# Layer 1's pair sums: sums of both ways on two column tiles of 64, the 65th column on four tiles of 32

## The chip, the cores and the metric

The kernel runs on one core of a Trainium2 chip. The core has a matrix engine (TensorE, in the profile "PE", with its weight loads as "PEld"), a vector engine (DVE), a scalar engine for activations (ACT), a general engine (POOL) and a queue that issues most transfers (SP). They run side by side, each in the order of its own queue, and wait for one another by semaphores. The metric is the device time of one execution in microseconds, the median of several runs. Lower is better.

## The reference, cut to what matters

The program has four graph layers over 4096 nodes with 64 features and a 4096 x 4096 adjacency. The change touches layer 1 alone, a hyperbolic layer:

```python
adj_att = jax.nn.sigmoid(left[:, None] + right[None, :] + b_att[0]) * adj
x_local = logmap(x[:, None, :], x[None, :, :], c)
support_t = jnp.einsum('ij,ijd->id', adj_att, x_local)
return proj(expmap(x, support_t, c), c)
...
# --- layer 1 (adj_preln) ---
h = jnp.maximum(_layernorm(x, axis=-1), 0.0)
x = x + _L1_gnn_ref(h, adj, L1_gnn_r, L1_gnn_w_att, L1_gnn_b_att)
```

`logmap(x_i, x_j)` is a vector of 64, made of `x_i` and `x_j` with factors that depend on the pair alone. So the sum over `j` needs, for each target `i`, a weighted sum over all sources `j` of 65 columns: the 64 features of `x_j`, scaled, and one scalar of `j`. The weight of a pair is the sigmoid, zero where there is no edge, times a factor of the distance. That factor is the same for (i, j) and (j, i), the sigmoid is not.

## The kernel before, in words

Layer 1's pairs are computed by `pairs_fast` (from L2106). The 4096 nodes stand in 8 groups of 512. A job is a pair of groups (gi, gj) with gj <= gi: 36 jobs, 8 of them on the diagonal. Two jobs make a batch, so there are 18 batches. The steps of a batch are:

- `scores` (L2211): for each block of 128 sources, two matmuls into the PSUM tile `pl` (L2194 for the missing edges, L2197 for the logits) and a sigmoid on ACT into `sg` (L2181 by way of L2204). An off-diagonal job has both directions, that is 8 sigmoids of 128x512, a diagonal job has 4.
- `distances` (L2217): four fp32 matmuls into `pu` (L2225), each read by DVE into `at` (L2232), then one DVE operation over the job's whole tile into `xt` (L2233).
- `factors` (L2236): a table load (L2239), and per job four ACT passes over 128x2048 elements (the logarithm of `xt`, the root, its inverse, the logarithm of `at`) with two DVE operations, L2247 between the root and the logarithm and L2252 after it. The tile `root` has one buffer. At its end `at` holds the job's factor F: 4 blocks of 128 sources (of gj) by 512 targets (of gi).
- `sums` (L2254): DVE multiplies the weights `w` of the direction gj to gi by F (L2260). Four fp32 matmuls with 65 weight columns add this to `acci` (L2262), which is kept over all gj of one gi. For an off-diagonal job F is also transposed, 16 transposes of 128x128 (L2277) into four `pf` tiles (two buffers). DVE multiplies each with the other direction's weights (L2280), and a matmul adds it to `accj` (L2281). DVE then adds `accj` to the rows of `VT` (L2288). On the diagonal DVE copies `acci` to `VT` (L2270).

`VT` is 65 x 4096. `acci` and `accj` have one PSUM buffer each. At the end each 65x128 block of `VT` is transposed by TensorE (L2312) and scaled by DVE into `VQ` (L2314). `finish` then works on `VQ`.

The loop at L2294 issues, for batch n, the factors of batch n+1, the sums of batch n, the scores of batch n+1 and the distances of batch n+2. A scheduler orders each engine's queue from there. Only the activations are kept in program order (`act`, L2180). So on TensorE and DVE the work of neighbouring batches lies mixed.

In the trace an fp32 matmul has two weight loads and two passes (288 of each for the 144 matmuls of `acci`), and it is listed with as many weight columns as it has. Where the output is a slice of 32 partitions such as `acc[k * O : (k + 1) * O, :]`, as in layer 0 at L1521 and L1396, the trace lists matmuls of 32 columns. The sums of layer 1 use one accumulator of 65 partitions:

```python
nc.tensor.matmul(
    accs[gi],
    lhsT=XQ[:, gj * GB + b, :],
    rhs=w[:, b, :],
    start=(gj == 0 and b == 0),
    stop=(gi == gj and b == GB - 1),
)
```

Of the kernel before, what the change touches and what calls it, by code (L numbers as in the profile page):

```python
# [9 lines left out]
F32 = mybir.dt.float32  # L10
# [8 lines left out]
ALU = mybir.AluOpType  # L19
# [5 lines left out]
P = 128  # L25
N = 4096
NB = N // P
D = 64
G = 512
NG = N // G  # L30
GB = G // P
# [799 lines left out]
def kernel(  # L831
# [24 lines left out]
    nc = tc.nc  # L856
# [7 lines left out]
    D1 = D + 1  # L864
# [10 lines left out]
    ident = cpool.tile([P, P], F32, name="ident")  # L875
# [35 lines left out]
    def load_adj(apool, g, q):  # L911
# [6 lines left out]
        )  # L918
        return t

    def over(col, width):

        return col.unsqueeze(2).to_broadcast([P, col.shape[1], width])
# [75 lines left out]
    with ExitStack() as l0:  # L999
# [143 lines left out]
        @contextmanager  # L1143
        def in_order():

            traced = nc.cur_bb.bb.instructions
            mark = traced[-1]
            yield
            start = next(k for k in reversed(range(len(traced))) if traced[k] is mark) + 1
            last = {}  # L1150
            for i in traced[start:]:
                if i.engine in (nc.vector.engine, nc.scalar.engine, nc.tensor.engine):
                    if i.engine in last:
                        tc.add_manual_dep(
                            i,
                            last[i.engine].name,
                            mybir.DependencyInfo(
                                mybir.DependencyClass.NoSync, mybir.DependencyReason.DATA
                            ),
                            reason="in_order",  # L1160
                        )
                    last[i.engine] = i

        def staggered(*streams):

# [259 lines left out]
        with ExitStack() as ha:  # L1425
            hp = ha.enter_context(tc.tile_pool(name="heads", bufs=2))
            work = ha.enter_context(tc.tile_pool(name="hwork", bufs=1))
# [32 lines left out]
            for hf in range(2):  # L1460
# [9 lines left out]
                for hd in range(NH):  # L1470
# [61 lines left out]
                    for j0 in range(0, NB, 2):  # L1532
# [19 lines left out]
                        for i, j in enumerate(range(j0, j0 + 2)):  # L1552
                            for n, (acc, y) in enumerate(parts):
# [3 lines left out]
                                    lambda k, i=i: B[:, i, k * G : (k + 1) * G],  # L1557
                                    start=j == 0 and (n == 0 or acc is not parts[n - 1][0]),
                                    stop=j == NB - 1 and (acc is not accB or n == len(parts) - 2 - spatial),
                                )  # L1560
                        for i, j in enumerate(range(j0, j0 + 2)):
                            for c in range(2):
# [4 lines left out]
                                    lambda k, i=i: C[:, i, k * G : (k + 1) * G],  # L1567
                                    start=j == 0 and c == 0,
                                    stop=False,
                                )  # L1570
                                if whole:
# [534 lines left out]
    def pairs_fast(es, VQ):  # L2106
# [14 lines left out]
        with ExitStack() as ss:  # L2121
# [27 lines left out]
            for dst, k in ((XA, 0), (LD, 1)):  # L2149
# [11 lines left out]
                for g in range(NG):  # L2161
# [4 lines left out]
                        ps,  # L2166
                        nc.scalar.copy,
                    )
        VT = fp.tile([D1, N], F32, name="VT")
        work = es.enter_context(tc.tile_pool(name="pfwork", bufs=2))  # L2170
        with ExitStack() as ss:
            ps_u = ss.enter_context(tc.tile_pool(name="ps_u", bufs=2, space=PSUM))
# [4 lines left out]
            def grp(g):  # L2177
                return slice(g * G, (g + 1) * G)
# [57 lines left out]
            def factors(batch):  # L2236
# [12 lines left out]
                for job in batch:  # L2249
                    at, xt = tiles[job]  # L2250
                    act(at, at, AF.Ln, bias=one_t, scale=1.0)
                    nc.vector.scalar_tensor_tensor(at, at, TMAX, xt, ALU.min, ALU.mult)  # L2252

            def sums(batch):  # L2254
                for gi, gj in batch:
                    F_ = tiles.pop((gi, gj))[0]
                    if gj == 0:
                        accs[gi] = ps_a.tile([D1, G], F32, name="acci", tag="acci")
                    w = sig.pop((gi, gj))
                    nc.vector.tensor_tensor(w, w, F_, ALU.mult)  # L2260
                    for b in range(GB):
                        nc.tensor.matmul(  # L2262
                            accs[gi],
                            lhsT=XQ[:, gj * GB + b, :],
                            rhs=w[:, b, :],
                            start=(gj == 0 and b == 0),
                            stop=(gi == gj and b == GB - 1),
                        )
                    if gi == gj:
                        nc.vector.tensor_copy(VT[:, grp(gi)], accs.pop(gi))  # L2270
                        continue
                    w = sig.pop((gj, gi))
                    accj = ps_a.tile([D1, G], F32, name="accj", tag="accj")
                    for t in range(GB):
                        pf = ps_f.tile([P, G], F32, name="pf", tag="pf")
                        for b in range(GB):
                            nc.tensor.transpose(  # L2277
                                pf[:, b * P : (b + 1) * P], F_[:, b, t * P : (t + 1) * P], ident
                            )
                        nc.vector.tensor_tensor(w[:, t, :], w[:, t, :], pf, ALU.mult)  # L2280
                        nc.tensor.matmul(  # L2281
                            accj,
                            lhsT=XQ[:, gi * GB + t, :],
                            rhs=w[:, t, :],
                            start=(t == 0),
                            stop=(t == GB - 1),
                        )
                    nc.vector.tensor_tensor(VT[:, grp(gj)], VT[:, grp(gj)], accj, ALU.add)  # L2288


# [13 lines left out]
                    distances(batches[n + 2])  # L2304

        nc.vector.tensor_scalar(pabs, pabs, sqc, 2.0, ALU.mult, ALU.mult)
        with tc.tile_pool(name="ps_vt", bufs=2, space=PSUM) as ps:
# [406 lines left out]
```

## Time and profile before

| What | us |
|---|---|
| median of 3 runs | 2257.73 (2257.61 to 2261.93) |
| profiled execution | 2264.45 |
| its span, first to last instruction | 2262.7 |
| pairs of layer 1, from the first `pu` to the last `VQ` | about 1240 to 1832 |
| DVE work of `finish` that follows directly | from 1832.06 |

Over the whole span PE is busy for 1938.4 us (86%), DVE for 1770.1 (78%) and ACT for 1589.8 (70%). The other stages are layer 0 before the pairs, and layers 2 and 3 after them. The pairs are a bit over a quarter of the span, and nothing of another layer runs beside them: `finish` reads `VQ`, whose last block comes from the last job. The pairs hardly use transfers (57 loads of 256 KB between 1280 and 1830 us).

In the profile's lines an engine's group gives the line, the operation, output and input tiles with their shapes, the count, busy time and mean duration, and the idle time just before. Durations of matmuls overlap: a pass of 512 columns is listed with its way through the array, and the next pass starts before it is over. So the distance from start to start is the cost of a pass, and it is shorter than the duration.

### The profile page before, as it was taken

Reading aid. Unit: us, or ns where it says so; the run is one execution under the profiler, and the core shown is the slowest. Engines: PE = TensorE matmul, PEld = TensorE weight load, DVE = VectorE, ACT = ScalarE, POOL = GpSimd, SP = SyncE. Lnnn points to the kernel's source line nnn. Section 1 sums busy time; section 2 is a strip of 40 time slices with the busy share of each in tenths; the row PEclk is TensorE's granted clock in tenths of the full one; section 3 lists DMA queues with packets and bytes.
Section 4 is the critical chain, followed back from the end, with each engine's and each line's share of the span. In section 5 each row is a group of like instructions: output and inputs, shape, how many; then the busy total and the mean of one; then the engine's idle time right before and its main releaser. Section 6 shows DMA issues by size and latency. Waiting matters only on the chain. (4 is left out here: it accounts for less than half of the span.)

```text
span 2262.7 us, 42590 instructions
## 1 busy us (share of the span) xinstructions
PE 1938.4 (86%) x18732; PEld 904.9 (40%) x18732; DVE 1770.1 (78%) x2074; ACT 1589.8 (70%) x1338; POOL 86.0 (4%) x124
## 2 busy tenths in 40 slices
PE   4989989999999999859992799999999933959998
PEld 3444444444444544423441244434344411434332
DVE  6689989987898899797657888888898889544552
ACT  4678878996898899467752888879788920114775
POOL 1000100100000000001101000000000000000000
PEclk8999999999999999879995899999999966965999
DMA  9945554352111020477530001100110005724993
GB/s 112 181 89 104 90 90 114 123 190 93 44 63 63 26 75 2 132 247 264 188 122 20 20 23 33 38 24 28 33 33 26 26 0 204 301 82 140 332 332 119
DMA packets 117002, 238.92 MB, mean 106 GB/s; under 512 B 11059, under 2 KB 84003, under 8 KB 102051
## 3 DMA queue, kind: packets, MB, share of 16 engines
q1 hardware_dynamic: 101990, 192.92, 24.6%
q0 software_dynamic: 14816, 43.18, 10.8%
q8 instruction: 148, 2.42, 0.4%
q14 instruction: 48, 0.39, 0.1%
HBM read 245.34 MB, written 49.46 MB: 130 GB/s over the span
## 5 line engine op out<-in xcount | busy, mean ns | idle before, releaser
L1185 ACT ACTIVATE st<-srow,nt 128x2048 int8<-128x2048 f32 x352 | 682.8, 1994 | 81.6 <-DVE B L1191 80.8
L1191 DVE TENSOR_TENSOR B<-st,mres 128x1024 int32<-128x1024 int32 x256 | 312.0, 1221 | 71.8 <-PE accC L1521 44.6
L1521 PE MATMUL accB<-B,ybh 128*32 128x512 fp8e4 x3072 | 340.5, 385 | 15.6 <-DVE B L1191 15.6
L1521 PE MATMUL accD<-B,ybh 128*32 128x512 fp8e4 x2048 | 302.6, 388 | 23.6 <-DVE h L1637 23.6
L1521 PEld LDWEIGHTS <-ybh 128*32 128x32 bf16 (+1 forms) x6656 | 197.5, 98 | 240.8 <-issue 79.8
L1521 PE MATMUL accC<-B,ycn 128*32 128x512 fp8e4 x2272 | 267.8, 380 | 1.2 <-issue 1.2
L1521 PE MATMUL accC<-mres,ych 128*32 128x512 fp8e4 x2272 | 268.0, 381 | 0.0
L1521 PE MATMUL accL<-B,ybh 128*32 128x512 fp8e4 x1536 | 221.4, 391 | 4.8 <-DVE h L1641 4.7
L1521 PEld LDWEIGHTS <-ych 128*32 128x32 f16 x4096 | 169.0, 99 | 116.5 <-issue 11.9
L929 DVE SCALAR_TENSOR_TENSOR raw<-raw 128x2048 f32<-128x2048 f32 x64 | 146.4, 2289 | 79.3 <-DMA raw<-in_adj_dram 79.1
L1179 DVE TENSOR_SCALAR st<-srow,nt 128x2048 uint8<-128x2048 f32 x160 | 205.6, 1285 | 2.5
L2181 ACT ACTIVATE sg<-pl,rb 128x512 f32<-128x512 f32 x256 | 163.6, 684 | 53.7 <-PE pl L2197 50.6
L1185 ACT ACTIVATE st<-srowo,nto 128x1024 int8<-128x1024 f32 x128 | 137.3, 1137 | 42.1 <-DVE B L1191 42.1
L2225 PE MATMUL pu<-XAf,LDf 66*128 66x512 f32 x288 | 151.4, 630 | 13.7 <-DVE at L2232 12.5
L2607 ACT ACTIVATE w3b<-pv 128x1024 int16<-128x1024 f32 x128 | 131.1, 1024 | 45.6 <-PE pv L2598 45.3
L1521 PE MATMUL accC<-C,ych 128*32 128x512 fp8e4 x1824 | 148.3, 393 | 1.4 <-DVE C L1199 1.4
L1199 DVE TENSOR_TENSOR C<-B,mres 128x1024 int32<-128x1024 int32 x114 | 139.6, 1225 | 3.6
L2262 PE MATMUL acci<-sg,VQ 128*65 128x512 f32 x288 | 137.8, 602 | 4.8 <-DVE sg L2260 4.6
L1521 PEld LDWEIGHTS <-ycn 128*32 128x32 f16 x2272 | 107.6, 97 | 64.0 <-issue 3.1
L2416 PE MATMUL nacc<-m,HH 128*128 128x512 fp8e4 x256 | 62.0, 391 | 74.6 <-ACT HH L2405 74.6
L2232 DVE TENSOR_SCALAR at<-pu 128x512 f32<-128x512 f32 x144 | 95.2, 685 | 26.2 <-PE pu L2225 26.2
L2194 PE MATMUL pl<-nm,noid 128*128 128x512 fp8e4 x256 | 101.0, 395 | 11.8 <-ACT sg L2181 11.7
(488 smaller groups left out, 3124.3 us busy)
## 6 DMA issues: line engine op xcount, KB each, us to landing
raw<-in_adj_dram SPq DMA_DIRECT2D x64, 1024.0 KB, 6.9
mo<-edges SPq DMA_DIRECT2D x32, 512.0 KB, 4.7
noedge<-nmo POOLq DMA_DIRECT2D x32, 512.0 KB, 4.3
nm<-noedge SPq DMA_DIRECT2D x64, 256.0 KB, 3.1
m<-edges SPq DMA_DIRECT2D x16, 1024.0 KB, 5.2
m<-edges SPq DMA_DIRECT2D x32, 512.0 KB, 5.0
srow<-srow_d SPq DMA_DIRECT2D x15, 1024.0 KB, 6.6
mres<-in_adj_dram POOLq DMA_DIRECT2D x8, 1024.0 KB, 35.7
```

The costliest lines, as they stand in the source:

```text
L929: nc.vector.scalar_tensor_tensor(raw, raw, 0.0, raw, ALU.is_gt, ALU.not_equal, accum_out=bad[:, c : c + 1])
L1179: nc.vector.tensor_scalar(st[:, i, :].bitcast(U8), srow, negs[:, i : i + 1], EDGE, ALU.is_gt, ALU.mult)
L1185: nc.scalar.activation(st[:, i, :], srow, AF.Sign, bias=negs[:, i : i + 1], scale=-1.0)
L1191: nc.vector.tensor_tensor(B.bitcast(I32), st.bitcast(I32), edges.bitcast(I32), ALU.bitwise_and)
L1199: nc.vector.tensor_tensor(C.bitcast(I32), B.bitcast(I32), edges.bitcast(I32), ALU.bitwise_xor)
L1521: ins = nc.tensor.matmul(acc[k * O : (k + 1) * O, :], lhsT=values, rhs=moving(k), start=start, stop=stop,)
L2181: tc.keep_in_program_order(nc.scalar.activation(*args, **kw))
L2194: nc.tensor.matmul(pl, lhsT=noid, rhs=nm[:, b, :].bitcast(F8), start=True, stop=False)
L2225: nc.tensor.matmul(pu, lhsT=LD[:, j * P : (j + 1) * P], rhs=XA[:, grp(gi)], start=True, stop=True,)
L2232: nc.vector.tensor_scalar(at[:, b, :], pu, UMIN, None, ALU.max)
L2262: nc.tensor.matmul(accs[gi], lhsT=XQ[:, gj * GB + b, :], rhs=w[:, b, :], start=(gj == 0 and b == 0), stop=(gi == gj and b == GB - 1),)
L2607: nc.scalar.activation(w, pv, AF.Relu)
```

## The change

The sums are put on column tiles. `acci` and `accj` become 128 partitions high. The 64 features of one direction go to one half of the array's columns and those of the other direction to the other half: for `accj` to partitions 0 to 63, for `acci` to 64 to 127. The 65th column is computed by separate matmuls with 32 weight columns (the last 32 of the 65, of which only the last counts), at four places: for `accj` in partitions 64 to 95 and 96 to 127, for `acci` in 0 to 31 and 32 to 63, one each for the even and the odd source block. For two source blocks there are so 4 matmuls of 64 columns and then 4 of 32, and `in_order` keeps these eight in this order among TensorE's instructions (others may stand between them). An off-diagonal job issues such a group after every second transposed tile. Before, the `acci` matmuls of a job stood free of the transposed tiles. A diagonal job gives two of its four sources to `accj` and two to `acci`. Its four matmuls of 32 columns give the odd blocks to `acci` and the even ones to `accj`.

`VT` becomes 128 x 4096. On the diagonal two copies of 64 partitions (L2291 and L2292 of the changed kernel) bring `acci` to the halves where `accj` has them, and `accj` is then added there as well. At the end a matmul with a constant `fold_v` takes the place of the transpose: it picks the 64 columns and adds the two partitions that hold the 65th.

`in_order` is moved out of another function unchanged. The diff, cut to its core:

```diff
-        VT = fp.tile([D1, N], F32, name="VT")
+        VT = fp.tile([P, N], F32, name="VT")
...
+            def add_up(acc, low, row, src, w, start, stop):
+                cols, r, n = (slice(0, D), low, D) if row is None else (slice(D1 - 32, D1), row, 32)
+                nc.tensor.matmul(
+                    acc[r : r + n, :], lhsT=XQ[:, src, cols], rhs=w, start=start, stop=stop
+                )
...
                     if gj == 0:
-                        accs[gi] = ps_a.tile([D1, G], F32, name="acci", tag="acci")
+                        accs[gi] = ps_a.tile([P, G], F32, name="acci", tag="acci")
+                    acci = accs[gi]
+                    accj = ps_a.tile([P, G], F32, name="accj", tag="accj")
                     w = sig.pop((gi, gj))
                     nc.vector.tensor_tensor(w, w, F_, ALU.mult)
-                    for b in range(GB):
-                        nc.tensor.matmul(
-                            accs[gi],
-                            lhsT=XQ[:, gj * GB + b, :],
-                            rhs=w[:, b, :],
...
                     if gi == gj:
-                        nc.vector.tensor_copy(VT[:, grp(gi)], accs.pop(gi))
-                        continue
...
+                        with in_order():
+                            for b in range(0, GB, 2):
+                                j = gj * GB + b
+                                add_up(accj, 0, None, j, w[:, b], b == 0, b == GB - 2)
+                                add_up(
+                                    acci, D, None, j + 1, w[:, b + 1], gi == 0 and b == 0, b == GB - 2
+                                )
+                            for b in range(GB):
+                                j = gj * GB + b
+                                r = b // 2 * 32
+                                if b % 2:
+                                    add_up(acci, 0, r, j, w[:, b], gi == 0, True)
+                                else:
+                                    add_up(accj, 0, D + r, j, w[:, b], True, True)
+                        accs.pop(gi)
+                        nc.vector.tensor_copy(VT[0:D, grp(gi)], acci[D : 2 * D])
+                        nc.vector.tensor_copy(VT[D : 2 * D, grp(gi)], acci[0:D])
+                    else:
+                        v = sig.pop((gj, gi))
+                        for t in range(GB):
...
+                            nc.vector.tensor_tensor(v[:, t, :], v[:, t, :], pf, ALU.mult)
+                            if t % 2 == 0:
+                                continue
+                            with in_order():
+                                for c in range(t - 1, t + 1):
+                                    add_up(accj, 0, None, gi * GB + c, v[:, c], c == 0, c == GB - 1)
+                                    add_up(
+                                        acci, D, None, gj * GB + c, w[:, c], gj == 0 and c == 0, False
+                                    )
+                                for k in range(2):
+                                    c = t - 1 + k
+                                    last = c + 2 >= GB
+                                    add_up(accj, 0, D + k * 32, gi * GB + c, v[:, c], t == 1, last)
+                                    add_up(
+                                        acci, 0, k * 32, gj * GB + c, w[:, c], gj == 0 and t == 1, False
+                                    )
                     nc.vector.tensor_tensor(VT[:, grp(gj)], VT[:, grp(gj)], accj, ALU.add)
...
+        fold_v = work.tile([P, D1], F32, name="fold_v", bufs=1)
+        nc.vector.tensor_copy(fold_v[:, 0:D], ident[:, 0:D])
+        nc.vector.tensor_tensor(
+            fold_v[:, D:], ident[:, D + 31 : D + 32], ident[:, P - 1 :], ALU.add
+        )
...
-                    nc.tensor.transpose(pt[:, b, :], VT[:, c : c + P], ident[:D1, :D1])
+                    nc.tensor.matmul(
+                        pt[:, b, :], lhsT=VT[:, c : c + P], rhs=fold_v, start=True, stop=True
+                    )
```

More of the change, by code (lines that the diff above doesn't have):

```diff
@@ L919, in load_adj, with in_order @@
         return t
+    @contextmanager
+    def in_order():
+        traced = nc.cur_bb.bb.instructions
+        mark = traced[-1]
+        yield
+        start = next(k for k in reversed(range(len(traced))) if traced[k] is mark) + 1
+        last = {}
+        for i in traced[start:]:
+            if i.engine in (nc.vector.engine, nc.scalar.engine, nc.tensor.engine):
+                if i.engine in last:
+                    tc.add_manual_dep(
+                        i,
+                        last[i.engine].name,
+                        mybir.DependencyInfo(
+                            mybir.DependencyClass.NoSync, mybir.DependencyReason.DATA
+                        ),
+                        reason="in_order",
+                    )
+                last[i.engine] = i
     def over(col, width):
@@ L1141, in behind @@
                 yield
[L1143 to L1162, printed above, removed]
         def staggered(*streams):
@@ L2257, in sums @@
                     if gj == 0:
-                        accs[gi] = ps_a.tile([D1, G], F32, name="acci", tag="acci")
+                        accs[gi] = ps_a.tile([P, G], F32, name="acci", tag="acci")
+                    acci = accs[gi]
+                    accj = ps_a.tile([P, G], F32, name="accj", tag="accj")
                     w = sig.pop((gi, gj))
                     nc.vector.tensor_tensor(w, w, F_, ALU.mult)
-                    for b in range(GB):
-                        nc.tensor.matmul(
-                            accs[gi],
-                            lhsT=XQ[:, gj * GB + b, :],
-                            rhs=w[:, b, :],
-                            start=(gj == 0 and b == 0),
-                            stop=(gi == gj and b == GB - 1),
-                        )
@@ L2269, in sums @@
-                    if gi == gj:
-                        nc.vector.tensor_copy(VT[:, grp(gi)], accs.pop(gi))
-                        continue
[L2272 to L2287, printed above, removed]
+                    if gi == gj:
+                        with in_order():
[18 more added lines that the diff above has]
+                        for t in range(GB):
+                            pf = ps_f.tile([P, G], F32, name="pf", tag="pf")
+                            for b in range(GB):
+                                nc.tensor.transpose(
+                                    pf[:, b * P : (b + 1) * P], F_[:, b, t * P : (t + 1) * P], ident
+                                )
[15 more added lines that the diff above has]
+                                    )
@@ L2306, in pairs_fast @@
         nc.vector.tensor_scalar(pabs, pabs, sqc, 2.0, ALU.mult, ALU.mult)
+        fold_v = work.tile([P, D1], F32, name="fold_v", bufs=1)
+        nc.vector.tensor_copy(fold_v[:, 0:D], ident[:, 0:D])
+        nc.vector.tensor_tensor(
+            fold_v[:, D:], ident[:, D + 31 : D + 32], ident[:, P - 1 :], ALU.add
+        )
         with tc.tile_pool(name="ps_vt", bufs=2, space=PSUM) as ps:
@@ L2311, in pairs_fast @@
                     c = (g * GB + b) * P
-                    nc.tensor.transpose(pt[:, b, :], VT[:, c : c + P], ident[:D1, :D1])
+                    nc.tensor.matmul(
+                        pt[:, b, :], lhsT=VT[:, c : c + P], rhs=fold_v, start=True, stop=True
+                    )
                 bs = slice(g * GB, (g + 1) * GB)
```

## The prediction, made before the changed kernel was run

> **What bounds the kernel now.** I read the pairs of layer 1 alone, since nothing else changes, first by windows from one table load of ACT (L2239) to the next, one batch each. The columns are start and end, the length, then busy time and instructions of PE, PEld, DVE, ACT and POOL, the granted clock, and transfers.
>
> ```profile
> 1494.60:1532.60 38.00, 35.71 (x106) 14.68 (x105) 33.68 (x31) 28.33 (x27) 0.00 (x0) 0.91 0.10 28
> 1532.60:1563.80 31.20, 30.34 (x109) 13.40 (x108) 26.05 (x26) 28.11 (x27) 0.00 (x0) 1.00 0.12 34
> 1563.80:1593.70 29.90, 28.08 (x93) 12.11 (x92) 24.88 (x21) 25.82 (x23) 0.00 (x0) 0.94 0.09 27
> 1240.00:1832.00 592.00, 549.07 (x1792) 234.07 (x1792) 504.91 (x444) 488.44 (x438) 0.00 (x0) 0.95 0.10 29
> ```
>
> A plain batch takes 31.2 us and PE works through 30.3 of it. The batches around a diagonal job take 37 to 38 us, and there DVE has 33.7. All three engines are near their limit: 549, 505 and 488 us of 592. Next the waits from 1280 to 1830 us (engine, line, whom it waited for, us, times, longest):
>
> ```profile
> ACT sg L2181 <- PE pl L2197: 48.6, 90, 1.8
> DVE sg L2280 <- PE pf L2277: 24.3, 20, 2.2
> ACT xt L2181 <- DVE xt L2233: 20.6, 8, 4.4
> DVE VT L2288 <- PE accj L2281: 17.2, 11, 2.3
> ACT root L2181 <- DVE at L2247: 7.8, 17, 0.9
> ```
>
> PE is what the others wait for most: ACT in its sigmoids, DVE for transposes and finished sums. But a faster PE soon meets DVE. Then the groups of the change, same window:
>
> ```profile
> L2262 PE MATMUL acci<-sg,VQ 128*65 128x512 f32 x288 | 137.8, 602 | 4.8 <-DVE sg L2260 4.6
> L2281 PE MATMUL accj<-sg,VQ 128*65 128x512 f32 x224 | 109.0, 603 | 0.4 <-DVE sg L2280 0.4
> L2288 DVE TENSOR_TENSOR VT<-VT,accj 65x512 f32<-65x512 f32 x28 | 19.0, 679 | 17.2 <-PE accj L2281 17.2
> L2270 DVE COPY VT<-acci 65x512 f32<-65x512 f32 x8 | 5.5, 683 | 2.2 <-PE acci L2262 2.2
> ```
>
> The 512 passes belong to 256 matmuls. They overlap: in the timeline their weight loads follow every 0.429 us (1500.18, 1500.61, 1501.04), so a matmul costs 0.857 us.
>
> Last, whether fp32 matmuls on column tiles run side by side. Layer 0 has one such place, L1396: 8 fp32 matmuls with 32 columns, four to a PSUM tile (timeline: start, us, what).
>
> ```profile
> 42.23 1.92 PE L1396 MATMUL prs<-FT,rs 96*32 96x512 f32 x16
> ```
>
> Eight in a row would take 8 x 0.857 = 6.9 us. Their 16 passes take 1.92, which is four steps of 0.43 and the last one's way out. So four stand side by side, though each brings its two passes one behind the other. What it costs to change the tiling shows in layer 0's output stage:
>
> ```profile
> 1154.00 1.03 PE L1948 MATMUL acco<-B,YBo 128*128 128x512 fp8e4 x4
> 1154.87 1.03 PE L1948 MATMUL acco<-C,YCo 128*128 128x512 fp8e4 x4
> 1155.82 0.39 PE L1961 MATMUL ddo<-B,YD 128*32 128x512 fp8e4 x1
> ```
>
> Four passes of full width take 0.87 us, 0.216 each. From there to the first of 32 columns it is 0.95, that is 0.31 for the last step: about 0.095 us for the change. Back again it is the same (last narrow pass at 1151.95, first wide one at 1152.27).
>
> **What the Trainium skill says.** "TensorEngine Tiling (Array Packing)", Key Properties: changing the tiling mode drains the TensorE, and different tiles work in parallel. The trace agrees with both, with 0.095 us and with L1396. "TensorE: Matmul & The Clock Gate", Part 3, What overlaps and what doesn't: matmuls keep strictly to program order. If the second pass of the first tile held up the next tile, the eight of L1396 would need nine steps, some 4.0 us. They took 1.92, so the measurement decides. The same page, Part 1: an idle PE falls to half its clock. The trace agrees: in the batches with a diagonal job the clock is 0.91, in plain ones 1.00.
>
> **The change, part by part.** PE, from the order of the built program.
> (a) Removed: 256 matmuls x 0.857 = 219.4 us.
> (b) Added: 256 of 64 columns in 128 pairs, 128 x 0.857 = 109.7, and 256 of 32 columns in 64 fours, 64 x 0.857 = 54.8. In the built order all fours but one stand together, and at least 122 of the 128 pairs.
> (c) Added: changes of tiling. I count 253 in the built order, 4 to a group of eight. 253 x 0.095 = 24.0 us. No row here shows a change between 64 and 32 columns: it costs between 0 and 0.17 (the way out of a pass, 0.592 less 0.429). I take 0.095. This sets the sum between 18 and 29.
> (d) The fold of `VT`: 32 transposes at a step of 0.062 become fp32 matmuls with two passes of 0.111 (the step of L2621's 64 columns), +5.1 us, most of it beside other work.
> PE's demand falls by 219.4 - 164.5 - 24.0 - 5.1 = 25.8 us. Counted by steps (`pl` 0.216 a pass, `pu` 0.857, `pf` 0.109) its whole demand goes from 504 to 478 us of 592.
>
> DVE. The diagonal jobs get one more copy and one more add: 8 x 0.683 + 8 x 0.679 = +10.9 us, and `fold_v` well under 1. Height in partitions costs nothing extra (a 65 x 512 copy and a 128 x 512 operation, L2280, both take 0.68).
>
> Only waits count, so I follow ACT, whose order doesn't change. A batch of ACT has a stretch of factors (18.4 us in the timeline from 1563.8, with half a us idle) and a stretch of sigmoids.
>
> Sigmoids: ACT does two in 1.27 us, 0.635 each. PE has two `pl` ahead. I summed PE's work between a batch's third `pl` and its last in both built orders: 164.2 us before, 145.9 after, since fewer of the sums fall there and the `pu` spread differently. ACT itself needs 14 x 0.635 = 8.9 us (16 sigmoids) or 6.4 (12). What PE has above that, batch by batch, is 24.4 us before and 9.0 after: -15.4 us. This is half of the wait of 48.6; the rest is the start of each stretch, and stays.
>
> Factors: here the new order costs. In DVE's queue `VT` += `accj` stands ahead of a batch's first L2247 in 13 of 18 batches, in 7 before, and no more than 1.3 us of DVE's work lies between it and the last product with `pf`. PE needs after this product a pair, a four, two changes and the way out: 0.86 + 0.86 + 0.19 + 0.17, with 0.1 to notice, some 2.2 us. So DVE stands until about 7.0 us after the table load, then adds (0.7) and starts L2247 at 7.7. Before, it started at 6.9 (1570.74, table load at 1563.81). The next root has one buffer and waits for it: +0.7 us in the 6 batches where this is new, and some +0.5 in the other 7, where the add waited for a single matmul and now waits for a group: 4.2 + 3.5 = +7.7. Queued behind the waiting add is all of DVE. PE behind `accj` waits as before for DVE's products, now with no `acci` to fill in.
>
> Diagonal batches: DVE gets 1.36 us more, while PE's sums of the diagonal job fall from 3.43 to 2.57 + 0.29. Here ACT waits up to 4.4 us for `xt`, whose `pu` stood behind eight passes of `acci`. I set them against each other: 0, between -1.5 and +1.4 each, 8 of them. The tail after the last factor: PE -1.8, DVE's two more operations +1.4, the fold +0.5: 0.
>
> Sum: -15.4 + 7.7 + 0 = -7.7, say -8. Against the profiled execution of 2264.45 that is 2256.4. The median of the runs lies 6.7 us below the profiled one, so 2249.7.
>
> **The rivals.** R1, PE's relief gets through: the add costs no wait, and the diagonal batches speed up too, by 1 us each: -15.4 - 8 = -23, 2234; with half of it -15, 2243. For it: PE is the releaser of 102 us of waits. Against: ACT and DVE have 28.1 and 26.1 us of work in a 31.2 us batch, dependent on one another. R2, DVE takes over: its 10.9 us come in full, -15.4 + 7.7 + 10.9 = +3.2, 2261; no change if a little less. For it: 33.7 of 38 us in the diagonal batches. R3, slower: the add at the head of DVE's queue. In the built order 11 of the 36 adds have at most 0.68 us of DVE's work between the last product and themselves. At 2.2 us each stands 1.5, and so do the three ops of each diagonal job. If this reaches ACT in all 18 batches at 1.5 (27 us) with half of the diagonal's 10.9, and PE gives its 15.4: +17; with two thirds of it +11, 2269. It decides from a delay of about 1 us a batch. Against: 17.2 us of such waits exist already and go. R4, the tiles of 64 don't run side by side: 512 x 0.857 + 24 - 219 = +243, or some +90 if the second passes block. L1396 speaks against it, with 32 columns and not 64.
>
> **How the numbers follow.** A measurement of this kernel can tell 0.2%, 4.5 us. Chances: forecast 0.40 (own range 2240 to 2258), R1 0.11, R2 0.17, R3 0.27, R4 0.05. Faster by over 0.2%: 0.36 of the forecast and R1, 0.47. Within: 0.04 and 0.16, 0.20. Slower: R3, R4 and the rest of R2, 0.33. The range 2234 to 2272 leaves out R4, the end of R1 and the far part of R3, under 0.2. Signs of both kinds hold much of it.
>
> **What would show it.** Right: L2260's passes of the changed kernel start in twos and fours within hundredths of a us, and a group of eight takes about 2.9 us; the wait of ACT for `pl` falls from 48.6 to 30 to 36; plain batches take about 30.5 us. The step on the add is right if L2318's waits for `accj` don't fall below 17 and the root's wait for DVE grows by some 8. Wrong: passes one behind the other (R4), DVE's idle time gone in the diagonal batches (R2), or waits of DVE for `accj` above 30 (R3).

## The result, and the profile after

| | us |
|---|---|
| changed kernel, median of 12 runs | 2255.46 (2249.20 to 2267.20) |
| kernel before, beside it, 12 runs | 2258.03 (2244.47 to 2261.93) |
| ratio, from all runs and not from the medians | 1.0002 (95%: 0.9979 to 1.0025) |
| profiled execution of the changed kernel, its span | 2256.87, 2254.9 |

The forecast was 8 us faster. The runs show no difference. The profile shows one: its pairs are shorter. The windows from one table load of ACT to the next, for the three batches that were shown of before, and then the whole of the pairs (columns: start and end, length, busy time and instructions of PE, PEld, DVE, ACT and POOL, granted clock, transfers):

```profile
1486.60:1520.10 33.50, 29.77 (x117) 10.85 (x116) 31.28 (x28) 28.30 (x26) 0.00 (x0) 0.95 0.11 32
1520.10:1552.50 32.40, 31.66 (x145) 11.43 (x144) 28.14 (x25) 28.07 (x26) 0.00 (x0) 1.00 0.11 33
1552.50:1581.40 28.90, 27.21 (x134) 10.68 (x132) 26.01 (x25) 25.57 (x23) 0.00 (x0) 1.00 0.10 28
1232.40:1815.20 582.80, 532.80 (x2336) 201.12 (x2336) 514.86 (x461) 486.95 (x436) 0.00 (x0) 0.96 0.10 29
```

The batch around a diagonal job fell from 38.0 to 33.5 us, and the plain one rose from 31.2 to 32.4. PE's busy time fell by 16 us from the 549.07 shown of before (by 11 from the 544.26 of another profile of it, see below), and DVE's rose by the 10 us of the extra copies and adds. The waits of the changed kernel from 1270 to 1815 us (engine, line, whom it waited for, us, times, longest):

```profile
ACT sg L2183 <- PE pl L2199: 41.3, 77, 3.4
DVE VT L2318 <- PE accj L2260: 21.6, 11, 2.4
ACT root L2183 <- DVE at L2249: 16.6, 17, 1.9
ACT xt L2183 <- DVE xt L2235: 12.1, 5, 5.5
DVE sg L2301 <- PE pf L2298: 10.3, 21, 1.7
PE accj L2260 <- DVE VT L2318: 7.1, 5, 3.8
```

The root's wait for DVE more than doubled (7.8 before), `VT`'s for PE grew a little (17.2 before, and 14.1 to 15.3 in three more profiles of it), DVE's for `pf` fell (24.3). The last line is new: PE waits for the add to give `accj` free. The lines shown of before start some 25 us after the first table load and so leave out a part of ACT's wait for `xt`. From the first table load to the end of the pairs ACT waits as follows (us, from the third profiles of both kernels, see below):

| ACT waits for | before | changed |
|---|---|---|
| `pl`, in the sigmoids | 44.7 | 42.0 |
| `xt`, in the first logarithm | 24.1 | 12.1 |
| DVE's addition of the root, before the next root | 8.5 | 17.3 |
| all | 77.3 | 71.4 |

So the wait for `xt` is what got shorter, and the root's wait took most of that back. And here is one group in the timeline of the changed kernel (start, us, what), with a pair of 64 columns and a four of 32:

```profile
1525.28 0.64 PE L2260 MATMUL accj<-sg,VQ 128*64 128x512 f32 x1
1525.29 0.64 PE L2260 MATMUL acci<-sg,VQ 128*64 128x512 f32 x1
1525.76 0.59 PE L2260 MATMUL accj<-sg,VQ 128*64 128x512 f32 x1
1525.77 0.59 PE L2260 MATMUL acci<-sg,VQ 128*64 128x512 f32 x1
1526.29 0.62 PE L2260 MATMUL accj<-sg,VQ 128*32 128x512 f32 x1
...
1526.31 0.62 PE L2260 MATMUL acci<-sg,VQ 128*32 128x512 f32 x1
1526.74 0.59 PE L2260 MATMUL accj<-sg,VQ 128*32 128x512 f32 x1
...
1527.29 0.55 PE L2298 MATMUL pf<-ident,at 128*128 128x128 f32 x3
```

The tiles do stand side by side: both first passes start within 0.01 us, then both second ones. So what was to be found out is where the pairs' gain went.

### The profile page after: what moved, and what is told of

Read it like the earlier page. It is cut to its first block, busy times and chain, and to the rows that moved or that the text cites. A ratio compares the mean times of both kernels' runs of the same rounds, so it can differ in the third digit from the quotient of the medians.

```text
span 2254.9 us, 43716 instructions
## 1 busy us (share of the span) xinstructions
PE 1920.0 (85%) x19276; PEld 870.7 (39%) x19276; DVE 1780.3 (79%) x2092; ACT 1588.5 (70%) x1338; POOL 86.2 (4%) x124
## 4 chain that ended last, share of the span: by engine, by line
PE 34%; DVE 15%; DMA 6%; ACT 4%; issue 4%; POOL 0%; SPq 0%; DVEq 0%; POOLq 0%; ACTq 0%
PE accj L2260 6%; DMA raw<-in_adj_dram 5%; PE acco L1948 5%; PE pu L2227 3%; PE nacc L2453 3%; PE pl L2196 2%; PE pf L2298 2%; PE pl L2199 2%; DVE at L2249 2%; DVE raw L950 2%; PE accC L1521 2%; DVE at L2254 1%; PE ddo L1961 1%; PE accB L1521 1%; PE tr L982 1%
## 5 line engine op out<-in xcount | busy, mean ns | idle before, releaser
L2260 PE MATMUL accj<-sg,VQ 128*64 128x512 f32 (+1 forms) x512 | 198.3, 615 | 18.6 <-DVE VT L2318 7.1
L2260 PE MATMUL acci<-sg,VQ 128*64 128x512 f32 (+1 forms) x512 | 197.7, 615 | 0.0
L2183 ACT ACTIVATE sg<-pl,rb 128x512 f32<-128x512 f32 x256 | 163.1, 684 | 47.3 <-PE pl L2199 43.3
L2644 ACT ACTIVATE w3b<-pv 128x1024 int16<-128x1024 f32 x128 | 131.1, 1024 | 54.6 <-PE pv L2635 54.3
```

The lines of the kernel that those rows point to most:

```text
L2183: tc.keep_in_program_order(nc.scalar.activation(*args, **kw))
L2260: nc.tensor.matmul(acc[r : r + n, :], lhsT=XQ[:, src, cols], rhs=w, start=start, stop=stop)
L2644: nc.scalar.activation(w, pv, AF.Relu)
```

## The experiments

Each theory bears the name that the expectation of its run gives it. They were named anew for each set of runs.

**Side by side needs the order.** Here `in_order` is left out in both places of `sums`, everything else is as in the changed kernel.

```diff
-                        with in_order():
+                        if True:
...
-                            with in_order():
+                            if True:
```

> The changed kernel without the fixed order of the eight matmuls of a group; the scheduler orders them freely. In the built order most matmuls of one accumulator then stand alone between others, and the tiling changes 423 times and not 253. Theory 1 (the matmuls gain only where both halves are issued together): the passes of a lone matmul take 0.86 us and not half of it, PE's demand grows by about 50 to 110 us and the pairs take 610 to 690 us. Theory 2 (the hardware brings halves together across other matmuls in the queue): the pairs take less than 590 us.

Measured: 2440.84 us, ratio 1.0847 (1.0821 to 1.0872), the pairs 767 us from the first table load instead of 569. Timeline:

```profile
1525.56 2.06 PE L2260 MATMUL accj<-sg,VQ 128*64 128x512 f32 x6
1527.55 0.66 PE L2298 MATMUL pf<-ident,at 128*128 128x128 f32 x4
1528.13 1.04 PE L2260 MATMUL acci<-sg,VQ 128*32 128x512 f32 x2
```

Most passes come without a partner. The first line shows both cases: it is one lone matmul of 64 columns (two passes 0.48 us apart) and then two of 32 that still found each other (they are printed as one group, under the shape of the first). Counted by starts within 0.03 us of each other, 394 of the 1024 passes have a partner here and 990 in the changed kernel. The pairs are even longer than the 610 to 690 us that were expected. The two passes of one matmul of 32 columns take 0.98 us alone (1528.13 to 1529.11), no less than one of full width with a change of tiling. A narrow matmul isn't cheaper by itself; only a neighbour makes it so.

**The add at the head of DVE's queue.** A rule of order puts a batch's first `VT` += `accj` behind the first `at` += `root` of the same stretch.

```diff
+                    r = nc.vector.tensor_tensor(at, at, root, ALU.add)
+                    if job == batch[0]:
+                        roots.append(r.ins)
...
+                    a = nc.vector.tensor_tensor(VT[:, grp(gj)], VT[:, grp(gj)], accj, ALU.add)
+                    if (gi, gj) == batch[0]:
+                        tc.add_manual_dep(
+                            a.ins,
+                            roots[-1].name,
...
+                                mybir.DependencyClass.NoSync, mybir.DependencyReason.DATA
```

> The changed kernel with one edge more on DVE: the add of accj to VT of a batch's first job is issued behind the first addition of the root (L2249 of the changed kernel), and not ahead of it. Theory 1 (the add at the head of DVE's queue delays the root and with it ACT, the +7.7 us of the prediction): ACT's wait for that addition falls from 15.9 us to 6 to 9, DVE's wait for accj from 21.6 to under 15, and the pairs get 4 to 9 us shorter than the 569.1 of the changed kernel. Theory 2 (the delay only moves: accj is then free later, and PE's next group waits for the add): ACT's wait falls, PE's wait for the add grows from 14 us to 20 or more, and the pairs stay within 3 us of 569.

Measured: 2255.89 us, ratio 1.0015 (0.9982 to 1.0047), the pairs 573.4. The waits, same columns as above:

```profile
DVE sg L2304 <- PE pf L2301: 27.9, 27, 2.5
PE accj L2263 <- DVE VT L2321: 19.6, 16, 3.8
ACT root L2183 <- DVE at L2250: 18.1, 17, 1.8
```

DVE no longer stands in front of the add: its wait for `accj` falls from 21.6 us to under 4. But the root's wait, which both theories had falling, stays (18.1), PE's wait for the add, which frees the one `accj` buffer, grows from 7.1 to 19.6, and DVE's for `pf` from 10.3 to 27.9. The delay moved, it didn't go, and in this one profile the pairs are 4 us longer than in the changed kernel.

**DVE's extra work on the diagonal.** In one kernel the add of `accj` on the diagonal is left out, so half of the diagonal jobs' sums is missing from `VT`. In the other the two copies run on ACT.

```diff
-                    nc.vector.tensor_tensor(VT[:, grp(gj)], VT[:, grp(gj)], accj, ALU.add)
+                    if gi != gj:
+                        nc.vector.tensor_tensor(VT[:, grp(gj)], VT[:, grp(gj)], accj, ALU.add)
```
```diff
-                        nc.vector.tensor_copy(VT[0:D, grp(gi)], acci[D : 2 * D])
+                        nc.scalar.copy(VT[0:D, grp(gi)], acci[D : 2 * D])
...
```

> The changed kernel without DVE's add of accj on the eight diagonal jobs: half of the sources of the diagonal's own group are left out of the sums. DVE has 5.4 us less to do. Theory 1 (DVE decides in the batches with a diagonal job, the rival in which DVE takes over): the pairs get 5 us or more shorter, 564 or less. Theory 2 (PE's order and ACT's chain decide there): 567 to 570.

> The changed kernel with the two copies of acci to VT on the diagonal done by ACT in place of DVE. DVE has 10.9 us less, ACT some 9 more. Theory 1 (DVE decides in the batches with a diagonal job): the pairs take 560 to 565 us. Theory 2 (ACT's chain decides): they take 572 to 580, since the copies stand in ACT's queue ahead of its factors. The total within 0.3% of before either way.

Without the add the pairs took 572.5 us in its one profile, 3 us more than with it and more than either theory had: the pairs don't wait for this add, half of DVE's extra work. (Its time of 2247.64 comes from layer 3, with 213.4 us; see below.) With ACT's copies: 2281.14 us, ratio 1.0130 (1.0077 to 1.0183), the pairs 593.8. The groups of that run, us busy and ns of one before the last bar:

```profile
L2183 ACT ACT_TABLE_LOAD x37 | 47.5, 1283 | 3.3 <-PE pl L2199 2.6
L2291 ACT COPY VT<-acci 64x512 f32<-64x512 f32 x8 | 4.7, 582 | 10.3 <-PE acci L2260 10.1
```

The copies themselves are short. But in the timeline sigmoids now stand among the logarithms and roots (at 1501.19 us, 1509.72 and 1516.93, each between two table loads), and L2183 has 37 table loads where the changed kernel has 18: 19 x 1.283 = 24.4 us, all of the loss. So the run says nothing on DVE, and the copies, the other half of its extra work, stay untested; it prices a torn stretch of activations.

**The same two kernels again.** Both unchanged, twice more, for the spread of the profiles.

> The kernel before, run and profiled once more, to see how much its stages vary by themselves. Theory A (the pairs really are 8 to 9 us shorter in the changed kernel, and the rest of the program varies by as much on its own): the pairs, from ACT's first table load of the pairs to the first operation of the step after them, take 577 to 578 us again, while layer 0 and layer 3 move by several us against the first profile. Theory B (layer 3 is longer in the changed kernel because of the change): layer 3 takes 224 to 226 us again. Theory C (the pairs vary by themselves): the pairs are off 577.6 by 4 us or more.

> The changed kernel once more. Theory A: the pairs take 568 to 570 us again and layer 3 anything from 222 to 236. Theory B: pairs 568 to 570, layer 3 233 us or more again. Theory C: pairs off 569.1 by 4 us or more. Total within 0.3% of before in A and B.

> The kernel before, profiled a third time. So far its pairs took 577.6 and 573.9 us with 65 and 55 us at half clock, layer 3 took 224.1 and 222.9. Theory A (the pairs of before are 4 to 9 us longer than those of the changed kernel): 573 to 578 again. Theory C (the pairs vary with the clock's windows, and the two profiles fell on the long side): under 572.

> The changed kernel, profiled a third time. So far its pairs took 569.0 and 569.2 us, layer 3 took 233.2 and 227.3 with 73 and 64 us at half clock from its start to the end of the record. Theory A with a chance clock in layer 3: pairs 568 to 570, layer 3 may be 223 to 226. Theory B (layer 3 is longer because of the change): layer 3 227 or more again.

Measured: before 2252.69 and 2246.80 (ratios to the kernel before beside it 0.9998 and 0.9984), changed 2252.91 and 2254.14 (0.9997, 0.9992, to at most 1.0025). By stages, in us, each in the order first, second, third profile. The pairs are from the first table load, which comes 13.5 to 13.8 us after the first `pu`, to `finish`:

| stage | before | changed |
|---|---|---|
| start to first `pu` | 1240.9, 1239.9, 1239.3 | 1232.4, 1233.4, 1232.5 |
| pairs | 577.6, 573.9, 573.8 | 569.0, 569.2, 569.7 |
| `finish` and layer 2 | 206.5, 206.4, 206.3 | 206.5, 206.5, 206.5 |
| layer 3, from its first `pv` | 224.1, 222.9, 226.2 | 233.2, 227.3, 230.7 |
| span | 2262.7, 2256.5, 2259.1 | 2254.9, 2249.8, 2252.8 |

The first row differs by more than the pairs do, 7.2 us between the means, though nothing was changed there. In the other profiles below and above it is 1231.4 to 1235.2 for kernels made from the one before and 1236.2 to 1239.7 for those made from the changed one, so the change doesn't move it; what does is open. The spans can't be compared as wholes.

The pairs are shorter in each profile of the changed kernel, and the profiles, but not the runs, say that the kernel is faster. The 166 runs of before, over all its measurements, explain this: they fall into two heaps, 74 around 2247.1 and 92 around 2260.0, with few near 2253. All three profiles of before are of the upper one. The 39 runs of the changed kernel can be read as one heap around 2255.2 and four runs from 2237.8 to 2246.9; the gap between them is 2.4 us, and with the cut at 2253 that divides the runs of before, 15 of the 39 would be below. The means of all runs are 2254.2 and 2253.8, a difference of -0.4 (95%: -2.5 to 1.7).

**What makes the diagonal batches shorter.** Two kernels from the one before. The first puts a diagonal job's first `acci` matmul behind the last `pu` traced ahead of it. The second traces the distances of batch n+2 ahead of the scores of batch n+1, where that has a diagonal job.

```diff
+                        if gi == gj and b == 0:
+                            tc.add_manual_dep(
+                                m.ins,
+                                last_pu[-1].name,
...
+                                    mybir.DependencyClass.NoSync, mybir.DependencyReason.DATA
```
```diff
                 sums(batch)
+                early = more and any(gi == gj for gi, gj in batches[n + 1])
+                if early and n + 2 < len(batches):
+                    distances(batches[n + 2])
                 if more:
                     scores(batches[n + 1])
-                if n + 2 < len(batches):
+                if not early and n + 2 < len(batches):
                     distances(batches[n + 2])
```

> The kernel before, with one more rule of order on TensorE: a diagonal job's first matmul of acci stands behind the last pu of the distances traced just before it. No work is added or left out. In the traces the four batches that hold a diagonal job's sums (periods from one table load to the next of 35.8, 38.1, 37.9 and 37.2 us in the kernel before, 32.9, 33.5, 33.4 and 33.0 in the changed one) carry the whole gain of the change. Theory D (place: ACT's logarithm waits for xt because the last two pu stand behind acci's passes): where the rule moves pu ahead, in the periods of 38, the period falls by 2 to 4 us each, the pairs as a whole by 4 to 9 us. Theory E (amount: TensorE has less to do for a diagonal job in the changed kernel, and its place doesn't matter): the pairs stay within 1.5 us of 573.8. Time of the whole: by D 0.1 to 0.4% below before, by E no difference.

> The kernel before, with the distances of batch n+2 traced ahead of the scores of batch n+1 where batch n+1 holds a diagonal job; nothing else. So the scheduler takes pu ahead of pl there. Theory D: the waits of ACT for xt fall from about 20 us to under 10, and the pairs by 4 to 9 us, unless the sigmoids, now behind pu, give it back (then the wait of ACT for pl grows by as much). Theory E: the pairs don't get shorter; with the sigmoids later they get 5 to 15 us longer.

The first: 2256.25 us, ratio 1.0009 (0.9983 to 1.0034), the pairs 576.4; of the two periods of 38 us one became 38.9 and one 36.1. ACT's wait for `xt` over the pairs is 23.3 us, 24.1 before: the rule hardly took it away, so this run doesn't say what the place is worth. The second is the telling one. Its diagonal batch and the two that follow, and two of its waits:

```profile
1486.00:1518.40 32.40, 30.12 (x88) 12.40 (x89) 27.39 (x25) 28.23 (x27) 0.00 (x0) 0.89 0.11 33
1518.40:1549.60 31.20, 30.21 (x108) 13.46 (x109) 26.68 (x26) 28.11 (x27) 0.00 (x0) 1.00 0.12 34
1549.60:1585.20 35.60, 33.57 (x107) 14.20 (x107) 30.96 (x27) 25.74 (x23) 0.00 (x0) 0.95 0.08 23
```
```profile
ACT sg L2181 <- PE pl L2197: 65.4, 88, 3.5
...
ACT xt L2181 <- DVE xt L2233: 1.0, 1, 1.0
```

The wait for `xt` went from 20.2 us to 1.0, and the diagonal batch is 5.7 us shorter, more than the change brought. But the sigmoids now wait 65.4 us for `pl`, 21 more, a later batch has 35.6 us instead of 28.3, and the pairs are at 575.5 as before. So here the place decided which batch pays, and the sum stayed: what Theory D named as its exception, and what Theory E says of the pairs, though not the 5 to 15 us more that E expected. That the changed kernel gains by the smaller amount of PE's work fits this, but no run changed the amount alone. Nor is the clock kept apart from it: TensorE is at half clock for 54.6 to 64.9 us of the pairs in the four profiles of before and for 47.8 to 51.2 in the three of the changed kernel. The 8.8 us between the means are worth at most 4.4 us of PE's work, and may be a cause of the shorter batches or follow from them. The median of the second kernel is nevertheless 2246.73, ratio 0.9975 (0.9957 to 0.9993), with unchanged pairs: 18 of its 22 runs are below 2252, in the lower heap.

**What the heaps are.** One more profile of the kernel before.

> The kernel before, unchanged, for one more profile. Its runs fall into two heaps, around 2246 and around 2259 us, and all three profiles so far are of the upper one. Theory C (the end of the program meets the clock differently from run to run): if this one is of the lower heap, the pairs are again 573 to 575 us and layer 3 is shorter by about 10 us (near 213 to 216 instead of 223 to 226), with less time at half clock there. Theory A (the pairs vary): the pairs are shorter by about 10 us and layer 3 is as before. If it falls into the upper heap it tells nothing new.

It was of the lower heap: 2249.8 us, span 2248.1, the pairs again 575.2, layer 3 217.2. Layer 3's first 50 us in three profiles: first before in the upper heap, then before in the lower one, then the changed kernel (windows, columns as above; the number after POOL is the clock):

```profile
2032.90:2082.90 50.00, 50.00 (x161) 24.44 (x160) 21.08 (x28) 20.48 (x36) 0.00 (x0) 0.50 0.42 148
```
```profile
2030.90:2080.90 50.00, 49.43 (x225) 22.31 (x228) 24.13 (x31) 31.92 (x47) 0.00 (x0) 0.84 0.60 214
```
```profile
2021.70:2071.70 50.00, 50.00 (x161) 24.50 (x160) 21.10 (x28) 20.50 (x36) 0.00 (x0) 0.50 0.42 147
```

PE is listed as busy nearly all the time in each, but at half clock it gets through 161 passes instead of 225, and ACT with it through 36 activations instead of 47. In the records of the clock this stretch at half speed begins 42 us ahead of layer 3's first `pv` and lasts 92.2 us in the upper heap and 58.0 in the lower one, in nothing between. It is 92.2 in all three profiles of the changed kernel, also in the one of 2251.72 us; of all the kernels here those profiled at 2247.5 to 2249.8 us have 58.0. From its beginning on TensorE has only small matmuls (17.9 of the 42 us ahead of layer 3), of which the last is shown, and then nothing (timeline of the changed kernel, the bracket is the idle time before):

```profile
1999.53 1.97 PE L2513 MATMUL pz<-w2f,cT 128*128 128x64 f32 x8 [0.67 <-ACT cT L983]
2018.70 1.01 PE L2571 MATMUL plate<-cnt,lat 128*128 128x512 bf16 x2 [17.21 <-issue]
```

The stretch isn't all of the distance between the heaps. From the mean of the first three profiles of before to the fourth the span falls by 11.3 us: 7.2 of it in layer 3 and 4.8 ahead of the first `pu` (1240.0 to 1235.2, with 163.8 us at half clock there in place of 174.1 to 180.9), while the stages between take 0.7 more. There is one profile of the lower heap of this kernel.

**The stretch, made shorter.** The changed kernel with 80 more matmuls there, whose result nobody reads:

```diff
+            warm = ps.tile([P, G], F32, name="warm", tag="misc")
+            for k in range(80):
+                nc.tensor.matmul(
+                    warm, lhsT=cnt16[:, 0, 0:P], rhs=cnt16[:, k % 2], start=True, stop=True
+                )
             w3 = lp.tile([D, D], F32, name="w3f")
```

> The changed kernel, with 80 more bf16 matmuls of 128x128 by 512 columns at the end of layer 2, whose result nobody reads (operands are the edge counts, the output a PSUM tile of layer 3's pool). In the built order 36 of them lie between the small matmuls of layer 2's last groups and 44 in the 17 us in which TensorE stands still ahead of layer 3. Nothing else is changed. In the profiles so far one stretch at half clock begins some 42 us ahead of layer 3's first pv and lasts either 92.2 us (all three profiles of the changed kernel, the long ones of before) or 58.0 us (the short one of before, with a layer 3 of 217.2 us in place of 223 to 226). Theory C (this stretch, and nothing in the pairs, makes the heaps, and eats the change's gain in layer 3): with TensorE kept at work the stretch is 58 us or shorter, layer 3 is at most 217 us in place of 227 to 233, the two heaps become one, and the median lies at 2235 to 2245, below before by 0.5 to 0.8%. Theory B (layer 3 is longer because of the change itself or of its transfers): layer 3 stays at 225 us or more whatever the clock ahead of it, and the median stays within 2250 to 2260, or gets up to 5 us longer by what the added matmuls delay in layer 2.

Measured: 2234.35 us (2230.05 to 2238.47 in 6 runs), ratio to the kernel before 0.9916 (0.9886 to 0.9946). The kernel before, beside it, took 2252.25 us in 11 runs. Its windows of the 42 us ahead of layer 3 and of the first 50 of it:

```profile
1978.20:2020.20 42.00, 31.82 (x192) 18.57 (x193) 29.62 (x61) 8.07 (x20) 4.00 (x6) 0.91 0.24 89
2020.20:2070.20 50.00, 49.43 (x225) 22.37 (x228) 25.09 (x32) 31.90 (x47) 0.00 (x0) 0.83 0.62 219
```

The stretch is 23.9 us long and begins 7.4 ahead of layer 3. Layer 3 takes 213.3 us, layer 2 with `finish` 199.2 instead of 206.5 (its eight passes `pz` take 1.08 us instead of 1.97), and the pairs are as they were, 569.8. The gap isn't quite filled: 43 of the matmuls take 9.4 us of it, then TensorE stands still for 7.7 us, and in these the stretch begins.

Theory B, that layer 3 is longer whatever the clock, is out. Of Theory C the stretch and layer 3 came as expected, the median just below its range. Two parts of it aren't shown. Six runs, within 8.4 us, can't tell that two heaps became one. And the kernel before wasn't run with these matmuls, so how much of the 0.84% is the change's own, and whether the stretch had hidden the change's gain, isn't measured. By the profiles the pairs are some 5 us of it (569.8 against 575.1 before).

## Why the prediction came out as it did

- **Side by side** (step (b), R4): right. A group of eight with nothing between took 2.86 us (1494.39 to 1497.25 in the third profile), 2.9 were forecast.
- **PE's relief of 25.8 us**: too large, by the term (c), the changes of tiling. From start to start, each pass counted at most with its own length, the sums fell from 223.2 to 196.8 us. But (third profiles) `pl` rose by 5.6, `pf` by 5.4 and the fold by 4.7, and `pu` fell by 1.1: together -11.8. Over the 164.5 us of steps of (b), the changed sums take 32.3 more, and with `pl` and `pf` 43.3, or 0.17 for each of the 253 changes instead of 0.095. Some of this is PE's way out ahead of a wait, so it is an upper value. The prediction had bounded the change at 0.17 and taken the middle.
- **The sigmoids, -15.4**: at most half of it came. ACT's wait for `pl` is 41.2 to 42.0, not 30 to 36. It was 48.6 in the profile that the forecast was made from, but 45.0 and 44.7 in the next two, and from these the fall is some 3 us. (The fourth shows 41.7, with 30 of the 512 `pl` passes missing from its record and 5 us of such waits put down to others.)
- **The add, +7.7**: right in size. The root's wait rose by 8.8, `VT`'s stayed between 17 and 30 (21.6). What the step didn't say is that the delay has no better place: one `accj` buffer ties the add, PE and `pf` together.
- **The diagonal batches, 0**: wrong, and this is where the pairs' gain came from. By periods from one table load to the next (third profiles), four of the eight took 149.0 us before and 132.9 after. The other four, three near the start and the last, took 5.4 us more together, and the ten batches without sums of a diagonal job 6.6 more, where some -0.7 for a plain batch was expected. Over the pairs ACT's wait for `xt` fell by 12.0 us. The pushed `pu` was named in the step, and then set off against DVE's two operations; leaving out one of these gained nothing.
- **The clock**: the prediction took the 0.91 of a diagonal batch for what an idle PE does. That batch shows half clock beside pauses and no more: PE's longest pause in it is 1.86 us, and the third row of its windows, with no sums of a diagonal job, has 0.94.
- **The sum for the pairs, -8**: measured -5.8 (means of the four profiles of before, 575.1, and three of the changed kernel, 569.3). It was near by luck: the sigmoids gave far less than forecast, the diagonal batches gave what was set at 0, and the two offset one another.
- **From the pairs to the time**: this step failed, and with it the gain of the whole. The prediction read the pairs "alone, since nothing else changes", and took the 6.7 us between profile and median as a constant. Three runs and one profile gave that constant, and all four happened to lie in the upper heap. In the profiles layer 3 is on average 230.4 us after and 224.4 before, with the same instructions: of the upper heap both, with some 10 us more at half clock later in the layer (63.4 to 72.8 us in layer 3 against 55.6 to 58.9). And by the times, with the four low runs taken as its lower heap, the changed kernel is in that heap in 4 of 39 runs, the one before in 74 of 166. So counted it is 4.8 us faster within the upper heap (2255.2 against 2260.0), about what its pairs gained.

No difference had a chance of 0.20, as the near end of R2 and of the forecast. It came from neither: leaving out one of DVE's extra operations gained nothing, and R3's delay cost what the forecast had given it. If the changed kernel meets the longer stretch more often, as the times suggest, why it does isn't settled. The starts of layer 3 at 2021.7 to 2022.6 us (changed) and 2030.9 to 2038.6 (before) don't order the cases: one kernel with 2027.2 and one with 2032.4 had 58.0, one with 2029.9 had 92.2. No run varied the start alone.

## What to carry to other kernels

Before a gain of under one per cent is forecast or believed, plot the single runs: two heaps can mean that a stage, perhaps one that the change doesn't touch, runs at two clocks, and a profile shows only one of them. Look for a TensorE that idles just ahead of a dense stage; here matmuls in that gap and in the pauses before it brought some 20 us to a kernel whose own change had brought 6 in its pairs. Price a change of tiling on both sides, for the narrow matmuls and for the wide ones that come after.

## What the runs showed of the hardware

- At the start of layer 3 PE was listed as busy in 50.00 of 50 us and stayed at half clock for all of them. The Trainium skill, "TensorE: Matmul & The Clock Gate", Part 1, has the clock released after some 3.4 us of sustained work. Here the lengths are multiples of the window of 3.413 us that it gives (92.2, 58.0 and, with the added matmuls, 23.9 us are 27, 17 and 7 of them), but in layer 3 the release came 50 or 16.6 us after its first `pv`. Of the 161 passes in those 50 us, 87 use only 32 rows (`pv` at L2627) or 64; whether that counts as too little work wasn't tried.
- Two column tiles each bring an fp32 matmul's two passes, and the partner's first pass starts 0.01 us after the first one's, ahead of the latter's second pass. The same page, Part 3, has matmuls strictly in program order; in the trace the passes of neighbours on different tiles overtake.
- The order of issue decides whether column tiles pay: without it the same 512 matmuls took 391.5 us of PE instead of 196.8 (counted as above), and the kernel took 8.5% longer than the one before.
